# A state-space scan with side work: a product of constants on idle TensorE steps, inputs asked for earlier, and a last carry that isn't copied

## The chip, the cores and the metric

The kernel runs on one core of one Trainium2 chip. The core has five engines that run side by side: PE (TensorE, matrix products), DVE (VectorE), ACT (ScalarE), POOL (GpSimd) and SP (SyncE, which issues nearly all transfers here). The metric is the device time of one execution in microseconds, 11,521.71 us as the median of three runs (11,514.94 to 11,524.55).

## The reference

Input `x` is 8 images of 64 x 64 x 96 in float32. Two layers follow each other, each a group normalisation and an added residual:

```python
x = x + _L0_conv_ref(_gn(x), ...)   # four-way selective scan
x = x + _L1_conv_ref(_gn(x), ...)   # upsample, MLP with a quadratic, low pass
```

Nearly all the time goes to the scan of the first layer. Of 192 channels and 16 states each, it runs over 4,096 positions in four directions:

```python
def step(h, inp):
    ul, dl, Bl, Cl = inp
    dA = jnp.exp(dl[..., None] * A)
    h = dA * h + (dl * ul)[..., None] * Bl[:, :, None, :]
    y = jnp.einsum('bkdn,bkn->bkd', h, Cl)
    return (h, y)
_, ys = lax.scan(step, h0, (u_t, d_t, B_t, C_t))
```

`ul` is the image after an input projection, a 3 x 3 depthwise convolution and SiLU; `dl`, `Bl` and `Cl` are projected from it. What stands around the scan is a projection and a gate before, a layer norm and an output projection after, and the second layer.

## The kernel before

**Tiles.** A tile of the scan is 8 channels x 16 states (128 partitions) by 1,024 positions. The 192 channels make `NT` = 24 tiles of a chunk; a direction has 4 chunks, an image 4 directions (taken in the order 1, 0, 2, 3), and there are 8 images: 128 chunks, 3,072 tiles. The loop near line 1115 handles one tile a step, with `i` its number; "step 20" means `i % 24 == 20`.

**A step.** For a tile, in its turn:

- `fetch` (L1001): SP asks for `dub`, 8 rows of `du` from DRAM, each broadcast to 16 partitions. It is done 6 steps ahead.
- `product_b` (L1007): POOL forms `bb = dub * br`, 3 steps ahead.
- `decay` (L1013, L1020): two PE products spread `dl` over the states into a PSUM tile `pd`, and ACT applies Exp in place. It is done one step ahead. There are two `pd` buffers.
- `scan` (L1027): DVE runs the recurrence. In most tiles it writes over `pd`; in a tile marked `by_pool` (one in three, in some chunks one in four) it writes an SBUF tile `h`.
- `product_c` (L1033): `hc = h * cr`, on DVE, or on POOL one step later in a `by_pool` tile.
- `hold` (L1037): the last column of `h` is copied to `carry`, on DVE, or on ACT for a `by_pool` tile. The next chunk of the same direction starts its scan from it; the first chunk of a direction starts from 0.0.
- `sums` (L1056, L1068): every second step, in odd ones, PE sums the states of two tiles into `py`, and every fourth pair adds what earlier directions left.

**Inputs of a chunk.** `prepare` makes `dl`, `br`, `cr` and `du` of the next chunk while the present one is scanned. Its `begin` (L913) asks for `u` by two transfers; `project` (L924) multiplies it on PE into `xd`; `delta` (L949 to L971) makes `dl`, multiplies `u` by it on POOL and stores `du` to DRAM. The `u` tile has one buffer. `begin` is queued in step 20, for the chunk after the next; the other parts are queued at step 0 of the next chunk and run in its first steps.

**Side work.** Everything else (the next image's convolution and gate, the last image's norm and output projection, the second layer) is cut into pieces that yield what they need of each engine, in microseconds as the author of the kernel reckons them. `Side.advance` gives each step an allowance for every engine (`CAPS`) and emits the pieces that fit, at most until it is spent. The PE time of `sums` is taken off as `taken` (0.95 for each). Pieces that need PSUM take one of three banks (`side0` to `side2`) with `bank` and return it with `give`; a returned bank is free from the next step on. Image 0 has only its own second half of the convolution and its gates beside it, and other images have most of it in some directions and little in others.

**Order.** It is written out by hand (`tc.manual_schedule()`): each engine runs its instructions in the order in which the loop emits them. So in a step PE gets `decay` of the next tile, then the side work, then `sums`.

## Time and profile before

| | |
|---|---|
| median of three runs | 11,521.71 us |
| the profiled execution, as timed | 11,526.07 us |
| its span, first to last instruction | 11,524.0 us |
| the scans, first start to last end | 143.7 to 11,239.9 us |
| mean granted PE clock | 0.913 |
| PE busy | 9,523.4 us (83%) |
| DVE busy | 10,419.6 us (90%) |
| ACT busy | 5,877.0 us (51%) |
| POOL busy | 10,195.9 us (88%) |

The page cuts the span into 40 slices of 288 us and shows for each engine the busy share in tenths; 9 is 90% or more. `PEclk` is the granted clock of PE in tenths of full speed. Before the first scan lies the convolution of image 0, and after the last one the tail of image 7, in which DVE and POOL have little or nothing to do. An engine's "idle before" is the time in which it had nothing to run, with the event that ended it; where an engine waits for several events, the one that came last by the profile is named, and it may stand for another of the same engine.

### The profile page before, as it was taken

Reading aid. Unit: us, or ns where it says so; the run is one execution under the profiler, and the core shown is the slowest. Engines: PE = TensorE matmul, PEld = TensorE weight load, DVE = VectorE, ACT = ScalarE, POOL = GpSimd, SP = SyncE. Lnnn points to the kernel's source line nnn. Section 1 sums busy time; section 2 is a strip of 40 time slices with the busy share of each in tenths; the row PEclk is TensorE's granted clock in tenths of the full one; section 3 lists DMA queues with packets and bytes.
Section 4 is the critical chain, followed back from the end, with each engine's and each line's share of the span. In section 5 each row is a group of like instructions: output and inputs, shape, how many; then the busy total and the mean of one; then the engine's idle time right before and its main releaser. Section 6 shows DMA issues by size and latency. Waiting matters only on the chain. (4 is left out here: it accounts for less than half of the span.)

```text
span 11524.0 us, 133552 instructions
## 1 busy us (share of the span) xinstructions
PE 9523.4 (83%) x42840; PEld 3036.7 (26%) x42840; DVE 10419.6 (90%) x8549; ACT 5877.0 (51%) x8210; POOL 10195.9 (88%) x4729
## 2 busy tenths in 40 slices
PE   7787768988789887888779897798977989788878
PEld 2121112322123222332223321232212322123225
DVE  5999999999999999999999999999999999899990
ACT  4455444556455454555545555454554546445443
POOL 4899998989989899999999998998999989899980
PEclk8898888999899998999889998899989999889987
DMA  6888898889988898898988889888898889988971
GB/s 150 205 196 221 201 217 202 209 217 233 221 201 212 214 229 217 207 215 216 235 204 215 213 210 240 201 213 212 218 234 205 214 212 232 218 200 211 230 189 47
DMA packets 1045088, 2401.01 MB, mean 208 GB/s; under 512 B 293948, under 2 KB 315708, under 8 KB 1044392
## 3 DMA queue, kind: packets, MB, share of 16 engines
q1 hardware_dynamic: 1040872, 2391.03, 84.3%
q8 instruction: 345, 5.65, 0.2%
q14 instruction: 351, 2.88, 0.1%
q10 hardware_dynamic: 3520, 1.46, 0.1%
HBM read 1929.05 MB, written 328.73 MB: 196 GB/s over the span
## 5 line engine op out<-in xcount | busy, mean ns | idle before, releaser
L1007 POOL TENSOR_TENSOR bb<-dub,br 128x1024 f32<-128x1024 f32 x3072 | 7174.9, 2358 | 357.9 <-DVE pd L1027 175.2
L1020 ACT ACTIVATE pd<-pd,neg_a 128x1024 f32<-128x1024 f32 x3072 | 3338.8, 1087 | 4952.4 <-PE pd L1013 4682.4
L1013 PE MATMUL pd<-dl,sel_b 64*128 64x512 f32 x12288 | 3833.8, 696 | 1781.3 <-DVE carry L1037 1556.1
L1027 DVE TENSOR_TENSOR_SCAN pd<-pd,carry,bb 128x1024 f32<-128x1024 f32 x1584 | 3722.4, 2350 | 328.0 <-ACT carry L1037 243.5
L1033 POOL TENSOR_TENSOR hc<-h,cr 128x1024 f32<-128x1024 f32 x960 | 2262.9, 2357 | 565.0 <-DVE h L1027 456.1
L1033 DVE TENSOR_TENSOR hc<-pd,cr 128x1024 f32<-128x1024 f32 x2112 | 2586.4, 1225 | 182.3 <-PE py L1056 43.5
L1013 PEld LDWEIGHTS pd<-dl,sel_b 64*128 64x128 f32 x12288 | 1053.2, 199 | 4243.7 <-issue 2837.3
L1056 PE MATMUL py<-hc,sel_r 128*32 128x512 f32 x12288 | 1839.2, 674 | 16.2 <-ACT yq L1089 15.5
L1027 DVE TENSOR_TENSOR_SCAN h<-pd,carry,bb 128x1024 f32<-128x1024 f32 x720 | 1684.3, 2339 | 51.6 <-ACT pd L1020 51.1
L1027 DVE TENSOR_TENSOR_SCAN pd<-pd,bb 128x1024 f32<-128x1024 f32 x528 | 1209.9, 2292 | 159.6 <-ACT carry L1037 129.8
L515 PE MATMUL pc<-pad,convr 96*128 96x512 f32 (+1 forms) x2304 | 867.9, 618 | 1.7 <-issue 1.7
L968 POOL TENSOR_TENSOR u<-dl,u 128x512 f32<-128x512 f32 x384 | 485.4, 1272 | 127.9 <-DMA br<-xd 127.8
L1027 DVE TENSOR_TENSOR_SCAN h<-pd,bb 128x1024 f32<-128x1024 f32 x240 | 547.4, 2281 | 17.3 <-ACT pd L1020 16.6
L1056 PEld LDWEIGHTS py<-hc,sel_r 128*32 128x32 f32 x12288 | 252.7, 113 | 1151.2 <-issue 838.8
L802 PEld LDWEIGHTS p<-w2q,mq 128*100 128x100 f32 x4800 | 454.5, 169 | 275.4 <-issue 212.4
L924 PE MATMUL px<-u,xp 64*64 64x512 f32 x1536 | 455.8, 650 | 78.6 <-DMA u<-u 78.6
L795 PE MATMUL ph<-xu,w 96*128 96x500 f32 x960 | 509.6, 635 | 10.9 <-ACT mq L796 6.1
L802 PE MATMUL p<-w2q,mq 128*100 128x96 f32 x4800 | 513.2, 259 | 2.7 <-ACT mq L796 2.7
L949 PE MATMUL pv<-xd,dt_w 64*64 64x512 f32 x1536 | 412.1, 629 | 9.4 <-ACT xd L934 9.2
L515 PEld LDWEIGHTS pc<-pad,convr 96*128 96x128 f32 (+1 forms) x2304 | 264.1, 163 | 570.2 <-issue 564.1
L796 ACT ACTIVATE mq<-ph,b 128x500 f32<-128x500 f32 x480 | 322.1, 678 | 73.2 <-PE ph L795 71.1
L1037 DVE COPY carry<-pd 128x1 f32<-128x1 f32 x2112 | 311.7, 148 | 0.0
(142 smaller groups left out, 6259.1 us busy)
## 6 DMA issues: line engine op xcount, KB each, us to landing
dub<-du SPq DMA_DIRECT2D x3072, 512.0 KB
u<-u SPq DMA_DIRECT2D x256, 384.0 KB
du<-u SPq DMA_DIRECT2D x768, 128.0 KB
y<-yq SPq DMA_DIRECT2D x768, 128.0 KB
br<-xd SPq DMA_DIRECT2D x256, 256.0 KB
cr<-xd SPq DMA_DIRECT2D x256, 256.0 KB
yp<-y SPq DMA_DIRECT2D x384, 128.0 KB
yp<-u SPq DMA_DIRECT2D x192, 128.0 KB
```

What stands on the lines that cost most here:

```text
L515: nc.tensor.matmul(t[rows].rearrange("p (i j) -> p i j", i=8), weights[:, cs], v["pad"][:, 8 * blk + kw : 8 * blk + kw + 8, kh : kh + H], ...
L795: nc.tensor.matmul(t[:, :px], w1[:, m, :], xu, start=True, stop=True)
L802: nc.tensor.matmul(t[:SIDE, C * i : C * i + C], sq[:, m, row], w2q[:, m, :], start=(m == 0), stop=(m == 2))
L924: nc.tensor.matmul(p[rows], xp[rows, k, q, :], v["u"][rows, q, :], start=(q == 0), stop=(q == 2), skip_group_check=True,)
L949: nc.tensor.matmul(t[rows], dt_w[rows, k, 64 * q : 64 * q + 64], v["xd"][rows], start=True, stop=True, skip_group_check=True,)
L968: nc.gpsimd.tensor_tensor(v["u"][:, q, :], got["dl"][:, q, :], v["u"][:, q, :], ALU.mult)
L1007: nc.gpsimd.tensor_tensor(t["bb"], t["dub"], t["got"]["br"], ALU.mult)
L1013: nc.tensor.matmul(pd[:, MB * hf : MB * hf + MB], sel_b[rows, 4 * t["s"] + t["j"]].rearrange("p n c -> p (n c)"), t["got"]["dl"][rows, t[" ...
L1020: nc.scalar.activation(pd, pd, AF.Exp, scale=neg_a[:, t["k"], t["g"] : t["g"] + 1])
L1027: nc.vector.tensor_tensor_scan(t["h"][:, ::step], pd[:, ::step], t["bb"][:, ::step], 0.0 if t["first"] else held, ALU.mult, ALU.add)
L1033: (nc.gpsimd if t["by_pool"] else nc.vector).tensor_tensor(t["hc"], t["h"], t["got"]["cr"], ALU.mult)
L1056: nc.tensor.matmul(py[r0 : r0 + 32], sel_r[:, t["j"], :], t["hc"][:, MB * hf : MB * hf + MB], start=(t["j"] == 0), stop=(t["j"] == 3 and t ...
```

## The change

Three things change. After the side work of a step, `turn_over` looks at the PE time that the step has spent (`spent`: what was taken for `sums`, plus what the pieces asked for). If it is under 0.5 and a bank is free, PE multiplies two constants (`ident` and the first half of `sel_b`, a 128 x 128 by 128 x 512 product) into that bank, and the bank is returned; nothing reads the result. `begin` of the chunk after the next is queued in step 16, not 20, from the third chunk on. And in a direction's last chunk `hold` returns at once, since no scan starts from that carry.

```diff
@@ class Side
+        self.spent = 0.0
@@ emit
+                self.spent += need.get("pe", 0.0)
                 for e, c in need.items():
                     self.left[e] -= c
@@ advance
-        self.caps = caps
+        self.caps, self.spent = caps, taken
@@ tiles
+                    tiles[-1]["last"] = n == NCH - 1
@@
+    def turn_over():
+
+        if side.spent < 0.5 and side.free:
+            n, p = side.bank("idle")
+            nc.tensor.matmul(p, ident, sel_b[:, 0:4].rearrange("p j n c -> p (j n c)"), start=True, stop=True)
+            side.give(n)
+
     def hold(t):
+        if t["last"]:
+            return
         end = T - 1 if t["k"] < 2 else 0
@@ the loop
-            if i % NT == 20 and i + 4 + NT < n:
-                nxt = tiles[i + 4 + NT]
+            ahead = 4 if i < 2 * NT else 8
+            if (i + ahead) % NT == 0 and i + ahead + NT < n:
+                nxt = tiles[i + ahead + NT]
                 begin, *side.later = prepare(nxt["b"], nxt["k"], nxt["i0"], nxt["got"])
                 side.urgent.append(begin)
@@ after side.advance(...)
+            turn_over()
             if ends:
                 sums(tiles[i - 3 : i - 1])
```

## The prediction

> **What bounds the kernel now.** I read the page's slices first, then windows by stage, then waits and timeline where a stage is slow.

> ```profile
> PE   7787768988789887888779897798977989788878
> DVE  5999999999999999999999999999999999899990
> ACT  4455444556455454555545555454554546445443
> POOL 4899998989989899999999998998999989899980
> PEclk8898888999899998999889998899989999889987
> ```

> From slice 2 to slice 38 DVE and POOL are both near nine tenths, and the PE clock is not constant. Scans run from 143.7 to 11239.9 us; the sum is made there. Two windows of equal length show what differs between stages (columns: length, then busy us of PE, PEld, DVE, ACT, POOL; clock; DMA share; GB/s):

> ```profile
> 1290.00:1376.00 86.00, 60.37 (x224) 14.14 (x222) 77.58 (x60) 34.17 (x46) 77.96 (x35) 0.80 0.80 195
> 2064.00:2150.00 86.00, 80.46 (x449) 32.18 (x449) 82.80 (x63) 50.22 (x73) 83.18 (x39) 1.00 0.89 214
> ```

> Where side work fills PE (second row) the clock is 1.00 and DVE works 82.8 of 86 us. Where PE has only the scan's own products the clock is 0.80, and DVE and POOL both lose 5 us. The timeline of the first window shows how (start, length, instruction, idle before it):

> ```profile
> 1306.41 1.13 PE L1013 MATMUL pd<-dl,sel_b 64*128 64x512 f32 x4 [1.49 <-DVE carry L1037]
> ...
> 1310.07 2.08 PE L1013 MATMUL pd<-dl,sel_b 64*128 64x512 f32 x4 [2.53 <-DVE carry L1037]
> 1312.18 1.09 ACT L1020 ACTIVATE pd<-pd,neg_a 128x1024 f32<-128x1024 f32 x1 [3.00 <-DVE h L1027]
> 1313.37 2.36 DVE L1027 TENSOR_TENSOR_SCAN pd<-pd,carry,bb 128x1024 f32<-128x1024 f32 x1 [1.19 <-ACT carry L1037]
> ...
> 1323.21 2.36 DVE L1027 TENSOR_TENSOR_SCAN pd<-pd,carry,bb 128x1024 f32<-128x1024 f32 x1 [0.24 <-ACT carry L1037]
> ```

> The step at 1306.41 is even: one pd product, then PE is idle for 2.53 us. The clock records then go to half from 1308.13 to 1314.96, and the next pd product takes 2.08 us, not 1.13. Exp (ACT, L1020) follows it and the scan follows Exp, so DVE stands 1.19 us; in the same place at full clock, at 1323.21, 0.24. (The wait is named after carry; by the program's semaphores the scan waits for Exp.) The loop is: DVE frees one of two pd banks, PE fills it, ACT does Exp, DVE scans. It sets the pace after a tile whose C product POOL does, since DVE then has one scan of 2.3 us to cover it.

> [...] only 1.00 and 0.50 occur, in multiples of 3.41 us, 301 half-clock spells of 2,012 us together, 1,861 among the scans. [...] I laid that 3.41 us grid over PE's busy time: of full-clock windows under 0.44 busy, 216 of 216 are followed by half clock; from 0.44 to 0.50, 72 of 107; above, 13 of 2,455. [...] a waiting px product holds back pd (below). So an added product stands ahead of the next pd product, and if it ran long, it would delay it.

> **Change, part 1: products of constants.** By the built order 392 of them are added, all in even steps 4 to 22 of a chunk; otherwise each compute engine keeps its order, less the copies below. 115 lie in image 0's 16 chunks (at most 10 a chunk), 36 in each of images 1 to 6, 61 in the last. The nearest row is the same shape in L1068, 1.12 us alone at full clock, 0.85 behind another product. Nothing reads the result; its bank returns at the next step, and what it waits for (mostly dl on DVE, one step old) is done by then. It fills 0.85 of PE's 2.5 us gap: hidden at full clock.

> What full clock is worth has two readings. (i) DVE's idle time before each scan, from the starts and ends in the trace, by the clock 2 us earlier: after another scan 1.35 us at half clock (103 cases) against 0.40 at full; after anything else 0.27 (323 cases) against -0.04 (starts overlap). 103 x 0.95 + 323 x 0.31 = 200 us. (ii) A line through the 128 chunks, time over the busier of DVE and POOL against half-clock time: 2.6 us + 0.16 per us; 0.16 x 1,861 = 300. I take 245.

> What share is won, the trace doesn't show: between nothing and all. My estimate: put 0.85 us of PE work right behind pd in the 392 steps, apply the limit 0.46 to each window of the trace, and count. Half-clock windows among the scans fall from 452 (by the same rule without the products) to 291, 36%. The rest are windows of 0.40 to 0.45, or steps that get no product. A kept clock also shortens three tiles from 10.8 us (1302.58 to 1313.37) to 9.8 (1313.37 to 1323.21), which lifts busy shares by a tenth; so I take 45%. 245 x 0.45 = **110 us**.

> Cost at half clock: the product takes about 2 us, and with pd's 2.08 fills 4.1 us, where DVE frees the next bank after 2.6 us if POOL has the tile (141 of the 392 steps). About 1.4 us each; if a fifth still run cold, 28 x 1.4 = 39 us at most. The added work also ends the cold spell, and waits of those tiles are in (i) already: I take **10 us** lost.

> **Part 2: input asked for earlier.** 124 of 128 u loads (two transfers each) leave SP at step 17 of a chunk, not 21; before them du has been stored (steps 8 to 11), so the single u buffer is free. They pass four steps of dub fetches and a pair of yp loads on SP; each pair costs SP 1.3 to 3 us, under its 4,669 us of waiting for POOL's bb at L1001. What it removes:

> ```profile
> 5768.92 2.54 SPq L913 DMA_DIRECT2D u<-u  x2
> ...
> 5777.60 1.97 PE L924 MATMUL px<-u,xp 64*64 64x512 f32 x2 [5.71 <-DMA u<-u]
> ...
> 5785.21 2.35 DVE L1027 TENSOR_TENSOR_SCAN h<-pd,carry,bb 128x1024 f32<-128x1024 f32 x1 [5.54 <-ACT pd L1020]
> ```

> The load is asked for at 5768.9 and PE stands for it until 5777.6, with pd behind. Four steps are some 14 us, so the 9 us fit. It happens once an image, in the second chunk of its first direction: 9.4 + 6.1 + 5.9 + 5.7 + 5.4 + 1.6 + 9.8 = 44 us of PE in images 1 to 7, some 54 on DVE. The two early waits of image 0 (10.8 and 22.4) remain, as those loads don't move. But POOL, with the last image's tail, is the bound there: in that chunk and the next it idles only 4.4 to 5.5 us of 195 (images 1, 4, 6). So a shorter DVE stall gives at most 5 us an image; I take 3, 7 x 3 = **20 us** (0 to 54).

> **Part 3: last carry.** 528 copies leave DVE and 240 ACT, a quarter of each.

> ```profile
> L1037 DVE COPY carry<-pd 128x1 f32<-128x1 f32 x2112 | 311.7, 148 | 0.0
> L1037 ACT COPY carry<-h 128x1 f32<-128x1 f32 x960 | 176.2, 184 | 96.7 <-DVE h L1027 95.7
> ```

> A DVE copy is busy 0.148 us, but the next instruction starts 0.07 after it (1306.11, 1306.18).[...] 528 x 0.068 = 36 us; the pd bank is also freed that much earlier. ACT has slack: nothing. In one direction of four the last chunk has POOL at 0.99: 36 x 3/4 = **27 us** (20 to 36; up to 78 if nothing overlapped).

> **Sum.** 110 - 10 + 20 + 27 = 147 us off the profiled execution's span of 11,524.0 (11,526.1 as timed), so 11,377; the median, 11,521.7, is 4 below the timed one: **11,375 us**.

> **Rivals.**
> - *The clock stays up* (0.20). For: every quiet even step gets a product, and the limit is sharp. Against: windows of 0.40 to 0.45 remain in the count. 245 + 25 + 33 = 303: 11,220 (11,180 to 11,290).
> - *The clock hardly gains* (0.20): drops move to the next thin window, or odd steps fall. Against: 216 of 216. Parts 2 and 3 alone: 11,475 (11,440 to 11,498).
> - *Slower* (0.07): the product itself becomes the wait. In-order PE meets it at half clock in the steps of POOL's tiles, at 1.4 us each, and the clock isn't won back. All 141 cost 197 us less the 47 of the other parts: 11,672; at 85 of them 119 - 47 = 72: 11,594. It is slower by over 0.2% from 50 of the 141 on.
> - *No effect* (0.04): POOL, 0.92 to 0.96 busy in quiet chunks too, takes all; within 11,500 to 11,545.

> My own case has 0.49, its own range 11,320 to 11,430. From 11,215 to 11,485 lie that case, most of the little-gain case and over half of the first rival: 8 in 10. About 0.2% (23 us) is what a measurement of this kernel can tell from no change; the cases give faster 0.87 (a tenth of the second rival falls inside the bound), same 0.06, slower 0.07.

> **What would show it.** Clock share 0.913 before should come to about 0.94 to 0.95, spells fewer than 301; in the quiet windows DVE should go from 77.6 to about 80 of 86 us. The px wait for u should drop to image 0's 33 us of 79; the pd scan's wait named after carry, 373 us before, should fall to some 280. DVE copies 1,584, and DVE busy 78 less. Wrong would be: a clock near 0.98 (first rival), a clock at 0.91 (second), idle products at 2 us with pd waiting behind them (third).

## The result and the profile after

The changed kernel takes 11,404.6 us (median of four runs, 11,399.85 to 11,421.22) against 11,523.1 of the kernel before in the same comparison (four runs, 11,514.94 to 11,539.29). The ratio is 0.9893, with an interval of 0.9881 to 0.9906, or some 120 us less. The prediction said 11,375 us, 147 less, with a range of 11,215 to 11,485 and faster at 0.87.

The profiled execution's span is 11,400.4 us, 123.6 below that of before. The scans now run from 142.6 to 11,118.9 us, where they ran from 143.7 to 11,239.9. That stretch is 119.9 us shorter, so nearly all of the gain lies in it. There DVE is idle for 638 us and was idle for 730; its busy time is 28 us less (10,391.8 against 10,419.6). 92 and 28 make 120: these are the two sizes to explain.

Two lines of the page's slices of the changed kernel, in tenths, answer to those of before:

```profile
POOL 4999999989999999999999998998989989999980
PEclk9999999999999999999999999999989999899998
```

The clock line had sixteen eights and a seven in 40 slices, and now has three eights; POOL's line has six eights, not ten. The granted clock is 0.947, where it was 0.913. By the clock records 206 spells at half clock remain of 301, and among the scans 1,072 us of 1,861.

Windows of the changed kernel at the same two places of the work, in the columns of the prediction (length, busy us of PE, PEld, DVE, ACT, POOL; clock; DMA share; GB/s):

```profile
1268.00:1354.00 86.00, 68.08 (x255) 16.33 (x248) 79.41 (x62) 35.63 (x49) 79.97 (x36) 0.90 0.80 201
2029.00:2115.00 86.00, 80.45 (x454) 32.55 (x452) 82.69 (x64) 50.21 (x73) 83.17 (x38) 1.00 0.86 212
```

In the quiet stretch the clock went from 0.80 to 0.90, DVE from 77.6 to 79.4 busy us of 86, and POOL from 78.0 to 80.0. The stretch that was at full clock is as it was. The timeline of the quiet one (start, length, instruction, idle before it):

```profile
1282.76 1.13 PE L1017 MATMUL pd<-dl,sel_b 64*128 64x512 f32 x4 [0.48 <-DVE carry L1050]
...
1283.82 1.12 PE L1043 MATMUL idle<-sel_b,ident 128*128 128x512 f32 x2
...
1286.42 1.13 PE L1017 MATMUL pd<-dl,sel_b 64*128 64x512 f32 x4 [1.47 <-DVE carry L1050]
...
1288.78 2.36 DVE L1031 TENSOR_TENSOR_SCAN pd<-pd,carry,bb 128x1024 f32<-128x1024 f32 x1 [0.25 <-ACT carry L1050]
```

These are the same tiles of the work as those from 1306.41 to 1313.37 in the prediction's timeline. In the even step the product of constants (L1043) follows the pd product at once. PE's gap ahead of the next pd product is 1.47 us, where it was 2.53: the product fills 1.06 of it. The clock stays full up to 1293.08, the next pd product takes 1.13 us and not 2.08, and the scan after a POOL tile's waits 0.25 us and not 1.19. The group of the new products by line and shape (count of records, busy us, mean ns of one, idle time before it):

```profile
L1043 PE MATMUL idle<-sel_b,ident 128*128 128x512 f32 x784 | 485.2, 704 | 0.0
L1050 DVE COPY carry<-pd 128x1 f32<-128x1 f32 x1584 | 234.0, 148 | 0.0
```

784 records are the 392 products, two for each. The last figure, 0.0, says that PE never waited for anything ahead of one. The copies on DVE are 1,584, as said.

The list of waits of the changed kernel (us in all, times, longest) shows where the earlier load went:

```profile
POOL bb L1011 <- DMA dub<-du: 244.6, 149, 9.0
DVE pd L1031 <- ACT carry L1050: 212.7, 367, 4.5
DVE pd L1031 <- ACT pd L1024: 121.8, 241, 3.4
DVE pd L1031 <- POOL bb L1011: 104.3, 53, 10.3
PE px L927 <- DMA u<-u: 36.0, 3, 24.8
```

PE's wait for u has fallen from 78.6 us to 36.0, which is image 0's. But POOL's wait for dub has risen from 173.4 to 244.6, and DVE's for POOL's bb from 28.1 to 104.3. DVE's waits for ACT, with both names taken together, have fallen from 373.3 + 78.5 = 452 to 335.

### The profile page after: what moved, and what is told of

It reads as the page before. It is cut to its first block, busy times and chain, and to the rows that moved or that the text cites. A ratio compares the mean times of both kernels' runs of the same rounds, so it can differ in the third digit from the quotient of the medians.

```text
span 11400.4 us, 134374 instructions
## 1 busy us (share of the span) xinstructions
PE 9630.9 (84%) x43624; PEld 3081.8 (27%) x43624; DVE 10391.8 (91%) x8021; ACT 5853.9 (51%) x7970; POOL 10192.8 (89%) x4729
## 5 line engine op out<-in xcount | busy, mean ns | idle before, releaser
L1011 POOL TENSOR_TENSOR bb<-dub,br 128x1024 f32<-128x1024 f32 x3072 | 7173.3, 2357 | 361.3 <-DMA dub<-du 244.6
L1017 PE MATMUL pd<-dl,sel_b 64*128 64x512 f32 x12288 | 3655.8, 666 | 1586.4 <-DVE carry L1050 1043.4
L1037 DVE TENSOR_TENSOR hc<-pd,cr 128x1024 f32<-128x1024 f32 x2112 | 2586.6, 1225 | 173.8 <-PE py L1069 34.2
L1037 POOL TENSOR_TENSOR hc<-h,cr 128x1024 f32<-128x1024 f32 x960 | 2261.4, 2356 | 440.6 <-DVE h L1031 344.2
L1017 PEld LDWEIGHTS pd<-dl,sel_b 64*128 64x128 f32 x12288 | 1005.0, 191 | 3959.7 <-issue 2335.2
L1069 PE MATMUL py<-hc,sel_r 128*32 128x512 f32 x12288 | 1739.9, 640 | 0.2
L1043 PE MATMUL idle<-sel_b,ident 128*128 128x512 f32 x784 | 485.2, 704 | 0.0
```

Source lines behind the costliest of these rows:

```text
L1011: nc.gpsimd.tensor_tensor(t["bb"], t["dub"], t["got"]["br"], ALU.mult)
L1017: nc.tensor.matmul(pd[:, MB * hf : MB * hf + MB], sel_b[rows, 4 * t["s"] + t["j"]].rearrange("p n c -> p (n c)"), t["got"]["dl"][rows, t[" ...
L1037: (nc.gpsimd if t["by_pool"] else nc.vector).tensor_tensor(t["hc"], t["h"], t["got"]["cr"], ALU.mult)
L1043: nc.tensor.matmul(p, ident, sel_b[:, 0:4].rearrange("p j n c -> p (j n c)"), start=True, stop=True)
L1069: nc.tensor.matmul(py[r0 : r0 + 32], sel_r[:, t["j"], :], t["hc"][:, MB * hf : MB * hf + MB], start=(t["j"] == 0), stop=(t["j"] == 3 and t ...
```

## The experiments

The theory: the clock gives some 100 us net, the copies 27 and the earlier load 20, and the three add up. The rivals: the clock gain isn't the products' work in PE but something beside it; the load's stall only moves; the product becomes the wait. Each experiment's ratio is to the kernel before on the same chip in the same comparison, with its interval; "half clock" is the time at half clock from the first scan to the end of the last, in its profiled execution.

| run | edit | median, us | ratio | clock | half clock, us |
|---|---|---|---|---|---|
| e1_product | products alone | 11,463.9 | 0.9923 [0.9903, 0.9943] | 0.945 | 1,096 |
| e2_carry | carry alone | 11,507.9 | 0.9969 [0.9957, 0.9982] | 0.911 | 1,926 |
| e3_ahead | earlier load alone | 11,538.2 | 0.9996 [0.9987, 1.0006] | 0.917 | 1,765 |
| e4_no_ahead | products and carry | 11,434.4 | 0.9902 [0.9883, 0.9921] | 0.945 | 1,117 |
| e5_small | all, products of 32 columns | 11,496.2 | 0.9969 [0.9959, 0.9979] | 0.916 | 1,799 |
| e6_more | all, 893 products | 11,333.0 | 0.9831 [0.9816, 0.9846] | 0.972 | 479 |
| e7_two | all, two products in each of the 392 steps | 11,391.5 | 0.9884 [0.9869, 0.9899] | 0.959 | 766 |
| e8_ahead12 | all, load asked for in step 12 | 11,435.5 | 0.9920 [0.9905, 0.9934] | 0.941 | 1,185 |
| e9_most | all, 2,053 products | 11,910.1 | 1.0321 [1.0304, 1.0338] | 0.978 | 379 |
| e10_more_no_ahead | 893 products, load as before | 11,373.5 | 0.9858 [0.9844, 0.9873] | 0.970 | 556 |
| e11_more_later | rule of 893, load as before, its readers 3 steps later | 11,282.1 | 0.9779 [0.9764, 0.9793] | 0.971 | 529 |
| e12_more_again | e6_more again, beside e10 and e11 | 11,342.1 | 0.9830 [0.9815, 0.9845] | 0.970 | 540 |

The kernel before had a median of 11,536.5 us beside e1 to e4, 11,533.4 beside e5 to e8, and 11,537.8 beside e9 to e12. One profile's half clock is not exact: the four kernels without a full product of constants (the kernel before, e2, e3 and e5) have 1,765 to 1,926 us.

### Each part alone

**The products** (against the changed kernel: the copies are back, and the load is asked for in step 20):

```diff
     def hold(t):
-        if t["last"]:
-            return
...
-            ahead = 4 if i < 2 * NT else 8
+            ahead = 4
```

> The kernel before with the products of constants alone. Theory: the clock share rises from 0.913 to about 0.945 and the time falls by about 100 us (85 to 130), to 11,420: nearly all of the measured gain of 118 us. Rival: the clock rises as much but POOL takes the time back, and the gain of the whole change comes from the carry and the input; then 20 us or less.

The ratio 0.9923 is 89 us of 11,536.5 (66 to 112). The half clock is down from 1,861 us to 1,096, by 41%. So the products alone make three quarters of the change, and each us of half clock that they save is worth 89 / 765 = 0.12 us.

**The last carry** (against the changed kernel: no product, load in step 20):

```diff
-            ahead = 4 if i < 2 * NT else 8
+            ahead = 4
...
-            turn_over()
```

> The kernel before, with the last carry of a direction not copied, alone. Theory: 528 DVE copies at 0.068 us less where POOL is the bound, 27 us (20 to 36). Rival: the pd bank freed 0.07 us earlier adds to it where the loop over PE and ACT sets the pace, or the copies do not overlap: 50 to 78 us. Second rival: nothing, because POOL is the bound there.

The ratio 0.9969 is 36 us (21 to 50), at a clock no better than before: 0.911. That is 528 x 0.068, the whole spacing of a copy to the next instruction.

**The earlier load** (against the changed kernel: no product, copies back):

```diff
     def hold(t):
-        if t["last"]:
-            return
...
-            turn_over()
```

> The kernel before, with the input asked for in step 16 instead of 20, alone. Recorded theory: 20 us faster (0 to 54). Revised after the trace of the changed kernel, where DVE waits 4 to 6.6 us for bb at the start of the second chunk of images 1 to 7, with POOL waiting for dub: the earlier load only delays the fetches behind it, and the time is the same within 10 us, or up to 30 us slower; the wait of px for u in images 1 to 7 is gone, and POOL's wait for dub is up by some 50 to 70 us from 173.

0.9996 [0.9987, 1.0006]: nothing, 15 us of gain at most. The waits of this run show why:

```profile
POOL bb L1011 <- DMA dub<-du: 216.8, 136, 8.4
DVE pd L1031 <- POOL bb L1011: 75.6, 42, 10.3
PE px L927 <- DMA u<-u: 34.5, 2, 23.7
```

PE waits for u 44 us less than before (78.6 to 34.5). POOL waits for dub 43 us more (173.4 to 216.8; 50 to 70 more were expected), and DVE for bb 48 us more (28.1 to 75.6). The stall that the prediction showed in detail, of 5.54 us on DVE, is the place to look. First more of the kernel before there:

```profile
5760.94 0.55 SPq L1001 DMA_DIRECT2D dub<-du  x1
...
5768.34 2.36 POOL L1007 TENSOR_TENSOR bb<-dub,br 128x1024 f32<-128x1024 f32 x1 [6.53 <-DMA dub<-du]
...
5771.73 2.35 DVE L1027 TENSOR_TENSOR_SCAN pd<-pd,carry,bb 128x1024 f32<-128x1024 f32 x1
...
5775.99 2.36 DVE L1027 TENSOR_TENSOR_SCAN pd<-pd,carry,bb 128x1024 f32<-128x1024 f32 x1 [0.53 <-POOL bb L1007]
...
5790.49 2.36 DVE L1027 TENSOR_TENSOR_SCAN pd<-pd,carry,bb 128x1024 f32<-128x1024 f32 x1 [2.94 <-ACT carry L1037]
```

Then the timeline of this run:

```profile
5736.75 1.26 SPq L916 DMA_DIRECT2D u<-u  x2
5741.27 2.83 SPq L631 DMA_DIRECT2D tz<-z  x2
...
5756.65 0.55 SPq L1005 DMA_DIRECT2D dub<-du  x1
...
5764.67 2.34 POOL L1011 TENSOR_TENSOR bb<-dub,br 128x1024 f32<-128x1024 f32 x1 [7.32 <-DMA dub<-du]
5767.05 2.36 DVE L1031 TENSOR_TENSOR_SCAN pd<-pd,carry,bb 128x1024 f32<-128x1024 f32 x1 [3.26 <-POOL bb L1011]
...
5772.29 2.36 DVE L1031 TENSOR_TENSOR_SCAN pd<-pd,carry,bb 128x1024 f32<-128x1024 f32 x1 [1.51 <-POOL bb L1011]
...
5776.92 2.35 DVE L1031 TENSOR_TENSOR_SCAN h<-pd,carry,bb 128x1024 f32<-128x1024 f32 x1 [0.95 <-POOL bb L1011]
...
5782.17 2.36 DVE L1031 TENSOR_TENSOR_SCAN pd<-pd,carry,bb 128x1024 f32<-128x1024 f32 x1 [2.90 <-POOL bb L1011]
```

The load is asked for early, among the transfers of the last image's tail (L631), and px doesn't wait for it any more. But the chunk's first four scans now stand 3.26, 1.51, 0.95 and 2.90 us for bb, 8.6 us together; in the trace of before the same four stand 0, 0.53, 5.54 and 2.94 us, 9.0 together. The stall moved; it wasn't removed.

The two traces also show where dub loses its time. The first dub of the second chunk leaves SP 44.41 us after the first chunk's tile 10 begins its scan (5756.65 against 5712.24), where it left 40.83 us after it (5760.94 against 5720.11). As a mean over images 1 to 7 it leaves 3.4 us later. But from this request to POOL's start it takes 7.9 us in the mean, as before (8.0). So the delay arises ahead of the request, in SP's order: the two requests for u take 1.3 us of it, and the rest goes to SP's longer waits ahead of the requests that follow.

**Products and carry without the load** (against the changed kernel):

```diff
-            ahead = 4 if i < 2 * NT else 8
+            ahead = 4
```

> The changed kernel with the input asked for in step 20 as before. If the earlier load is worth 20 us as recorded: 20 us slower than the changed kernel, 11,425. If the stall only moved from u to dub: 11,405 or faster, down to 11,380.

0.9902, or 113 us. On top of the products the copies are again worth 30 us (11,463.9 to 11,434.4). The whole change has 0.9893 [0.9881, 0.9906] in its own comparison; 10 us lie between the two, so the load's share on top of the other parts is 10 us, which the intervals don't tell from nothing. The parts alone, 89 + 36 + 5, come to 130, against 123 for all: they add up.

### Is it the work in PE?

**A product of 32 columns** in place of 512, in the same steps, with the same bank and the same waits (against the changed kernel):

```diff
-            nc.tensor.matmul(p, ident, sel_b[:, 0:4].rearrange("p j n c -> p (j n c)"), start=True, stop=True)
+            nc.tensor.matmul(p[:, 0:32], ident, ident[:, 0:32], start=True, stop=True)
```

> The changed kernel with the product of constants cut to 32 of its 512 columns, at the same places in PE's order, with the same banks and waits. Theory[...]: the clock falls back to about 0.915 and the time is that of the carry and the input alone, 35 to 45 us under before, 80 us over the changed kernel. Rival (what helps is a product at all, or the changed turns of the banks): the clock stays at 0.945 and the time at the changed kernel's, within 20 us.

The clock line of this run's page, and the group of its products:

```profile
PEclk8888888989889998999989998899988999899988
L1043 PE MATMUL idle<-ident 128*128 128x32 f32 x784 | 173.2, 305 | 0.0
```

The eights are back, the clock is 0.916, and the half clock 1,799 us. The ratio 0.9969 is that of the carry alone. So neither the order of the instructions nor the bank that is taken gives the gain: in the same steps and banks, products that kept PE busy for 173 us in all left the clock at 0.916, and those of the changed kernel, with 485 us, have it at 0.947. What differs is the time for which PE works.

**How much more is there?** A bound of 1.0 in place of 0.5 gives every step a product that has at most one `sums` product or a small piece (893 products); two products in each of the 392 steps; and a bound of 2.0 (2,053 products). Against the changed kernel:

```diff
# e6_more, and again e12_more_again
-        if side.spent < 0.5 and side.free:
+        if side.spent < 1.0 and side.free:
# e7_two: a second product after the first
+            nc.tensor.matmul(p, ident, sel_b[:, 0:4].rearrange("p j n c -> p (j n c)"), start=True, stop=True)
# e9_most
-        if side.spent < 0.5 and side.free:
+        if side.spent < 2.0 and side.free:
```

> The changed kernel with the product also in steps that spent up to 1.0 (odd steps with sums alone, even steps with one side product): 893 products, not 392. Theory: half-clock time among the scans falls from 1,072 us to about 400, at 0.16 us for each 60 to 110 us faster than the changed kernel, clock 0.97 or more. Rival (PE's order becomes the wait): pd, sums and the product fill 2.8 us where DVE frees a bank after 2.6 us in POOL's tiles; 0 to 60 us slower than the changed kernel in spite of the higher clock.

> The kernel with 893 products (steps that spent up to 1.0, input asked for in step 16) once more, as the base of the other three of this chip: about 0.983 of the kernel before, 11,335.

> The changed kernel with two products of constants one behind the other in the same 392 steps, 1.7 us at full clock. Theory: the clock rises a little (0.95 to 0.96), and in the 141 steps of POOL's tiles pd waits 0.2 to 0.3 us for PE: within 30 us of the changed kernel. Rival (the product is what the recorded forecast calls slower: 1.4 us for each of POOL's tiles): 40 to 150 us slower.

> 2,053 products: in steps that spent up to 2.0, nearly every step with a free bank. Theory: the clock comes to 0.98 or more, but with up to 2 us of sums and side work, pd and the product PE has 4 us of work a step where DVE frees a bank after 2.6 to 3.7, so the product itself is the wait: slower than the base by 20 to 150 us. Rival (only the clock counts): the last 480 us at half clock go, at 0.12 us each up to 58 us faster than the base.

With 893 products the half clock falls to some 500 us and the ratio to 0.9831 and 0.9830 in two comparisons. Against the changed kernel that is 72 us more for about 560 us of half clock, 0.13 for each, the same price as in e1. The gain from the clock is thus nearly proportional over the whole span measured, and the changed kernel takes some 60% of what 893 products take. Two products in the same steps bring the clock to 0.959 but only 0.9884, not to be told from the change's 0.9893: 300 us of half clock fewer should have been worth some 35.

With 2,053 products the clock is the highest of all, 0.978, and the kernel is 3.2% slower. Against e12 that is 568 us, where 20 to 150 were expected: the direction was foreseen and the size was not. The waits of DVE in it, and a stretch of its timeline:

```profile
DVE pd L1031 <- ACT carry L1050: 431.7, 446, 2.8
DVE pd L1031 <- ACT pd L1024: 320.8, 478, 4.9
```

```profile
3030.50 1.13 PE L1017 MATMUL pd<-dl,sel_b 64*128 64x512 f32 x4 [1.41 <-DVE carry L1050]
3031.56 1.12 PE L1043 MATMUL idle<-sel_b,ident 128*128 128x512 f32 x2
3032.61 1.06 PE L1069 MATMUL py<-hc,sel_r 128*32 128x512 f32 x8
3033.61 1.13 PE L1081 MATMUL py<-yp,d_diag 128*128 128x512 f32 x2
3033.80 2.28 DVE L1031 TENSOR_TENSOR_SCAN h<-pd,bb 128x1024 f32<-128x1024 f32 x1
3034.66 1.13 PE L1017 MATMUL pd<-dl,sel_b 64*128 64x512 f32 x4
...
3037.03 2.30 DVE L1031 TENSOR_TENSOR_SCAN pd<-pd,bb 128x1024 f32<-128x1024 f32 x1 [0.95 <-ACT carry L1050]
```

PE goes through 3030.50 to 3034.66 without a gap. DVE's last reading of the pd bank is a copy at 3033.73, ahead of the scan at 3033.80. The pd product that refills it starts at 3034.66, behind two products of `sums` that the product of constants has pushed back by 1.1 us, and the scan at 3037.03 stands 0.95 us. Over the whole trace PE is still at work in 1,435 of the steps with a product of constants when DVE frees the bank, and DVE stands 556 us before the scans of the tiles that refill it. DVE's waits for ACT, under both names, are 752 us, where e12 has 262, and DVE's idle time among the scans is 1,097 us against 582. This is the mechanism of the prediction's slower rival, with the clock up: a product in the wrong step is itself the wait.

### The load again

**Asked for still earlier** (against the changed kernel):

```diff
-            ahead = 4 if i < 2 * NT else 8
+            ahead = 4 if i < 2 * NT else 12
```

> The changed kernel with the input asked for in step 12, not 16. If the input in step 16 is worth nothing because it stands among the transfers of the last image's tail at the end of the first chunk, ahead of the fetches of dub: 10 to 25 us faster than the changed kernel, POOL's wait for dub under 245 us. If the stall goes wherever the load goes, or the load in step 12 waits on SP for du to be stored: the same within 15 us, or slower.

0.9920 [0.9905, 0.9934], where the change has 0.9893 [0.9881, 0.9906], with POOL's wait for dub at 236.5 us. To ask earlier still doesn't help, and rather costs; part of the 31 us may be the clock's, with 1,185 us at half clock against 1,072.

**The load at a high clock**: 893 products with the load in step 20 (e10), and the same with its readers later instead of the load earlier (e11). In e11 `side.urgent += side.later`, which queues the projection of u and what follows it, moves from step 0 of the chunk to step 3; with that the rule picks 771 steps. Against e12:

```diff
# both
-            ahead = 4 if i < 2 * NT else 8
+            ahead = 4
# e11_more_later
-            if i % NT == 0:
+            if i % NT == 3:
```

> 893 products, input asked for in step 20 as in the kernel before. Theory (POOL and the transfers of the tail bound the start of an image, so the earlier input only moves the stall): within 15 us of the base. Rival (with the clock high the stall for u is no longer covered): 25 to 55 us slower than the base.

> 893 products, input asked for in step 20, and the products that read it put off from step 0 to step 3, so that the load has three more steps and no transfer is moved ahead of others. PE's wait for u in images 1 to 7 should be gone as in the base, and POOL's wait for dub lower, 175 to 210 us, not 235. If the moved transfer cost what the removed wait gave: 15 to 40 us faster than the base. If POOL's own work is the bound there: within 15 us of the base.

The waits of e10 for u and for dub, then the same two of e11:

```profile
POOL bb L1011 <- DMA dub<-du: 218.9, 167, 8.8
PE px L927 <- DMA u<-u: 120.2, 14, 23.9
```

```profile
POOL bb L1011 <- DMA dub<-du: 169.3, 111, 8.1
PE px L927 <- DMA u<-u: 10.8, 1, 10.8
```

e10 is 31 us slower than e12, though both have the same clock and half clock (556 and 540 us). So with the clock high the earlier load is worth some 31 us, where it was worth nothing alone; the intervals of the two just meet (0.9844 and 0.9845), so the size is loose. The theory recorded for e10 (within 15 us) fails, and the size is that of its rival (25 to 55 us). DVE's waits for ACT before the scans into `h`, the kind that the stall of 5.54 us is, fit that: 84 us in e10 and 20 in e12. e11 is 60 us faster than e12 and 91 faster than e10, with 122 fewer products than either. Both expected ranges, 15 to 40 us and within 15, were too low. It takes away the wait for u but for 10.8 us ahead of the first scan, and POOL's wait for dub is 169 us and not 219 or 249. With 11,282.1 us (0.9779) it is the fastest version, 2.2% below the kernel before and some 1.2% below the change as made. By the profiles, its gain over e12 lies at the two ends. Image 0 takes 1,306 us against 1,332, most of it in its first direction (328.4 against 345.3). Image 7 takes 1,348 against 1,380 us, and for that no cause is shown, since the later start also packs the side work in another way. In images 1 to 6, each of which has the stall for u that the load was moved for, the two are within some 7 us of each other, and e11 is 7 us ahead over all six. So e11 shows that this version is faster, and not that the moved load costs 60 us.

## Why the prediction was right, and where not

The forecast's sign, its main mechanism and its range were right; the gain of some 120 us is four fifths of the 147.

**The clock (110 - 10 = 100 us).** Right. Measured alone, 89 us, with 100 inside its interval. The share of half clock won back was put at 45% and was 42% (1,861 to 1,072; 41% in e1). A microsecond of half clock was worth 0.12 to 0.13, where the middle of the two readings was 245 / 1,861 = 0.13; reading (i), 200 us, gives 0.11 and reading (ii), 300 us, gives 0.16, so the price that DVE's idle time gave was nearer than the fitted line. The rival in which the clock hardly gains falls by e1 and e5. The rival in which it stays up falls by the 1,072 us that remain; it needed over twice as many products (e6: 479 us), and even then 195 us and not 303 came out.

**What the product costs.** Hidden, as said, but not 0.85 us long: behind a pd product it takes 1.06 us at full clock (0.86 is what the second product takes in e7, behind one of its own kind). At half clock it takes 2.07 us, as said, in the 18 cases that lie wholly in it; 41 of the 392 begin there, a tenth where a fifth was allowed for. In 14 of POOL's steps with a product PE was still at work, at half clock, when DVE freed the bank, and the next pd product came 1.5 us late. But DVE didn't stand before the scans that needed it, so the 10 us put down for this are not seen. The slower rival's place was right and its point not reached: e9 shows it from another side, at full clock, in steps that hold `sums` products.

**The last carry (27 us).** The mechanism was right, and the term was a quarter too small: 36 us [21, 50], and 30 on top of the products. The full spacing of 0.068 us a copy counts. The reduction by a quarter, for a last chunk with POOL at 0.99, isn't seen, though the interval would allow it. The sign "DVE busy 78 less" was wrong: it is 28 less. A copy's 0.148 us of busy time overlaps the next instruction, which starts 0.07 us after it, and busy time counts overlapped time once; so 528 x 0.068 = 36 was the number to name. What such a copy cost here, 0.068 us of 0.148, is less than half of its busy time.

**The earlier load (20 us).** This is the step that failed. "So a shorter DVE stall gives at most 5 us an image; I take 3" let the load through without a price, because "each pair costs SP 1.3 to 3 us, under its 4,669 us of waiting". That sum of waits is one over the whole span, and at the end of an image's first chunk SP had no such slack. The wait for u fell as said, to 34 to 36 us, and what the load is moved past, the dub transfers, came late: alone, 44 us less on px stand against 43 more on POOL. The prediction had written POOL as the bound of those chunks, and had not asked what POOL itself waits for there. Nor did the transfer itself become slower in e3: the first dub of the second chunk takes 7.9 us from request to use, as before (8.0), and is asked for 3.4 us later. The load's worth also depends on the clock: 5 us alone, 10 on top of the change's products, 31 beside 893 of them.

**The named waits.** The wait named after carry should have fallen to some 280 us: it is 212.7. Part of it only changed its name, since a POOL tile in a last chunk has no carry copy on ACT now, and the wait for Exp after it is then named after pd: with the carry alone (e2) the two are 276.8 and 199.4 us. Both names together fell by 117 us, from 452 to 335.

**The sum.** 89 + 36 + 5 = 130 from the parts alone and 123 by the ratio of the whole, against 100 + 27 + 20 = 147. Of the 17 us by which the parts fell short, the load is 15 and the clock 11, and the copies gave 9 back; the 7 between 130 and 123 is within what the intervals leave open. That the total came as near as it did is partly luck, since the copies were put too low and the load too high.

## What to carry to other kernels

Where PE's clock falls in stretches in which PE paces nothing by its amount of work, count in the trace after how busy a stretch it falls, and try a filler product in the thin ones. In this kernel 288 of the 301 falls before came after 3.41 us windows under 0.50 busy. 392 products alone gave 89 us, 893 gave 72 us more than the change as made, and with 2,053 the kernel was 568 us slower than with 893: in 1,435 steps PE was still at work when DVE freed the bank. So look at the gap ahead of the next product that another engine needs (2.53 us in the timeline of before, of which one product fills 1.06). Before a load is moved ahead, name which transfers it passes and which engine waits for them (here dub and POOL, which waited 43 us more in e3); moving its reader back instead is worth a trial (the version with that was the fastest here, though most of its lead lies where the load's place does not explain it). And an instruction that overlaps its follower is priced by the spacing of the starts, not by its busy time: 528 copies, each 0.148 us busy and spaced by 0.068, gave 36 us here.

## What was not expected of the hardware

**Half clock was left only after windows at least 0.83 busy.** On the same grid, a half-clock window that was under 0.8 busy was followed by another in 183 of 183 cases before and 75 of 75 after, and one over 0.9 busy by another in 71 of 363 and 50 of 253. Even of the windows busy throughout, 57 of 305 were followed by another before. Of the 300 returns to full clock before, none came after a window less than 0.83 busy. Of the 301 falls before, 216 came after windows under 0.44 busy, 72 after windows up to 0.50, and 13 above. Why falls and returns lie so far apart, no trace here shows.

**A product of 32 columns did not hold the clock.** It took 305 ns a record where one of 512 took 704, and there were 1,799 us of half clock, within the 1,765 to 1,926 of the four kernels without a full product.

**The clock could be had nearly whole, and not the time.** At 0.972 the kernel gained 195 us, at 0.978 it lost 372. And at 0.959 (e7) it gained no more than can be told from 0.947, though PE had nothing to do but constants in those steps. In its trace the second product does hold the next pd product back: in 115 of POOL's 141 steps PE was still at work at full clock when DVE freed the bank, and pd came 0.72 us late on average. But DVE didn't stand before the scans there. So why the higher clock brought so little stays open; the intervals would allow some 30 us of gain.
